# First causal attention of a layered kernel: its row sums' reciprocals spread through DRAM, TensorE's order in groups of up to three steps, and other places for its first tiles and for later layers' loads

## The chip, the cores and the metric

The kernel runs on one core of a Trainium2 chip. Its time is the device time of one execution in microseconds; the time before is the median of three executions.

## The reference

Eight layers are applied to x of 4 batches, 1024 positions and 128 features, each with a residual: an attention, a mixture of experts, a gated attention unit, the same mixture again, a state space layer, a gated feed-forward layer, a second attention, and the feed-forward layer again. The change is in the first attention, with 16 heads of 64 features, all in float32:

```python
q, k, v = split_heads(x @ Wq), split_heads(x @ Wk), split_heads(x @ Wv)   # x is layer-normalized
scores = einsum('bhid,bhjd->bhij', q / sqrt(64), k)       # 1024 x 1024 for each batch and head
attn = softmax(where(causal, -inf, scores), axis=-1)      # key j > query i is masked
out = einsum('bhij,bhjd->bhid', attn, v)                  # heads joined, then @ Wo + bo
```

## The kernel before

**Tiles.** Positions lie on the 128 partitions, in blocks of 128 (`NC` = 8 for each batch). The work is done for a pair of heads `n` at a time: 8 pairs for each of 4 batches, 32 in all, since the features of two heads fill 128 partitions. For a pair, `gq` (0 to 3) counts units of two query blocks (`Q` = 2). A unit has `gq` + 1 steps, and each step takes two key blocks.

**First stage** (`probabilities`, L344 to L387). For each query block TensorE makes scores `s` (L358) of both heads against up to 512 keys, into a PSUM tile of two banks (`ps_s`, 2 buffers). VectorE adds the mask, negates, writes `p` and keeps the row's least value (L364). ScalarE takes the exponential in place and sums the row (L373). When a unit's two query blocks are done, VectorE takes the reciprocals `r` of the sums (L379), and POOL splits them into three bfloat16 parts (L382 to L385).

**Second stage** (`outputs`, L410 to L471). For each step TensorE transposes the blocks of `p` into `t` (L422, a PSUM tile of one bank for each key block, 2 buffers). ScalarE and VectorE copy them to `pt` (L427, L429). TensorE multiplies them with the values into `o` (L460): the first head's features on the lower 64 partitions, the second's on the upper. The reciprocals must lie along `o`'s free dimension and be the same on all 64 partitions of a head: TensorE transposes `parts` (L442), ScalarE copies them (L443), and TensorE multiplies them with a selection matrix `sel` (L452) into the second half of `o`'s bank. ScalarE copies that (L468), and VectorE multiplies it with the product (L469).

**The order.** `pe = k.order()` pins TensorE's instructions to the order in which the code issues them; the other engines' order is a scheduler's. In each step of `outputs` come the transposes of this step, one piece, the spread of the reciprocals if it is waiting, `ahead()`, and then the products of the step before. `ahead()` issues scores of later units until they lead by 20 blocks of 128 x 128 (`LEAD`). A piece is a small job from a list: the projections of pair n + 2 to q, k (L288) and v (L299), the product with Wo for pair n - 1 (L326), and transposes of the normalized x (L268) and of the result (L336). Each piece uses the one PSUM bank of `ps_m`, as the transpose of `parts` does. A batch is normalized (`normalize`, L104 to L119) two pairs before its first.

**The start.** The constructors of all layers run first. They issue the loads of all weights, nearly all on SP's queue, with W1 and W2 of the mixture (2 MB each) among them. Three integer weights of the feed-forward layer are loaded to tiles that are given back at once, and converted on VectorE (L1299). ScalarE and VectorE make `a` of the state space layer (L1046, L1047). The attention's own tiles are taken after that, and `a_one` lies where the given-back tiles lay; the first tiles taken from it are `ident_b`, `mask` and `sel`.

Of the kernel before, what the change touches and what calls it, by code (L numbers as in the profile page):

```python
# [61 lines left out]
class Kernel:  # L62


    def __init__(self, ctx: ExitStack, tc: tile.TileContext, ins: dict, out):
# [13 lines left out]
        self.turn = 0  # L79

    def load(self, pool, name, shape=None, src=None, dtype=F32, engine=None):

        ap = self.ins[name] if src is None else src
        t = pool.tile(list(shape or ap.shape), dtype, name="w_" + name)
        (engine or self.nc.sync).dma_start(t, ap)
        return t
# [15 lines left out]
    def normalize(self, out, in_, n=NC):  # L104
# [4 lines left out]
        for c in range(n):  # L109
            nc.vector.bn_stats(stats[:, c, :], in_[:, c, :])  # L110
        for c in range(n):
            nc.vector.bn_aggr(mv[:, c, :], stats[:, c, :])
        rstd = self.small.tile([P, n], F32, tag="rstd", name="rstd")
        nc.scalar.activation(rstd, mv[:, :, 1], AF.Sqrt, bias=self.eps)
        nc.vector.reciprocal(rstd, rstd)
        for c in range(n):
            nc.vector.tensor_scalar(
                out[:, c, :], in_[:, c, :], mv[:, c, 0:1], rstd[:, c : c + 1], ALU.subtract, ALU.mult
            )  # L119
# [68 lines left out]
class AttentionA:  # L188
# [10 lines left out]

    Q = 2  # L200
    NQ = NC // 2
    NS = 3
# [12 lines left out]
    def __call__(self, start=None):  # L215
        k, tc, nc = self.k, self.k.tc, self.k.nc
        wq, wk, wv, wo, bo = self.wq, self.wk, self.wv, self.wo, self.bo
        Q, NQ, NS, NP = self.Q, self.NQ, self.NS, HEADS // 2
        scale = 1.0 / math.sqrt(DH_A)
        with self.stack as ctx:  # L220
            one = ctx.enter_context(tc.tile_pool(name="a_one", bufs=1))
            sb = ctx.enter_context(tc.tile_pool(name="a_sb", bufs=2))
            ps_s = ctx.enter_context(tc.tile_pool(name="a_ps", bufs=2, space=PSUM))
            ps_t = ctx.enter_context(tc.tile_pool(name="a_pt", bufs=2, space=PSUM))
            ps_o = ctx.enter_context(tc.tile_pool(name="a_po", bufs=1, space=PSUM))
            ps_m = ctx.enter_context(tc.tile_pool(name="a_pm", bufs=1, space=PSUM))
            pe = k.order()

            ident_b = one.tile([P, P], BF16, name="ident_b")
            make_identity(nc, ident_b)  # L230

            mask = one.tile([P, T], BF16, name="mask")
            nc.gpsimd.memset(mask, 0.0)
            nc.gpsimd.affine_select(
                out=mask[:, T - P :], in_=mask[:, T - P :], compare_op=ALU.is_ge, fill=MASKED, base=0,
                pattern=[[-1, P]], channel_multiplier=1,
            )

            rows = NS * 2 * Q
            sel = one.tile([DH_A, Q, P], BF16, name="sel")  # L240
            nc.vector.memset(sel, 0.0)
            for i in range(Q):
                for h in range(2):
                    to = sel[:rows, i, h * DH_A : (h + 1) * DH_A]
                    for part in range(NS):
                        at = (part * 2 + h) * Q + i
                        nc.vector.tensor_tensor(
                            to, to, ident_b[:rows, at : at + 1].to_broadcast([rows, DH_A]), ALU.add
                        )

            turned_parts = [one.tile([DH_A, P], BF16, name=f"turned_parts{n}") for n in range(2)]
            for t in turned_parts:
                nc.vector.memset(t, 0.0)
# [3 lines left out]
            def normalized(b):  # L257
                xl = one.tile([P, NC, C], F32, tag="xl", name="xl")
                k.normalize(xl, k.xb(b))
# [3 lines left out]
                xts[b] = sb.tile([P, T], F32, tag="xt", name="xt")  # L263

                def turned(h):
                    ps = ps_m.tile([P, 512], F32, tag="m", name="ps")
                    for c in range(4):
                        pe(nc.tensor.transpose(ps[:, c * P : (c + 1) * P], xl[:, h * 4 + c, :], k.ident))  # L268
                    k.evacuate(xts[b][:, h * 512 : (h + 1) * 512], ps)
# [74 lines left out]
            def probabilities(n, gq):  # L344

                q, kk = pairs[n]["q"], pairs[n]["k"]
                p = one.tile([P, 2, Q, (gq + 1) * Q * P], F32, tag=f"p{gq}", name="p")
                tops = sb.tile([P, 2, Q, 2], F32, tag="tops", name="tops", bufs=3)
                sums = sb.tile([P, 2, Q], F32, tag="sums", name="sums")
                for i in range(Q):  # L350
                    ib = gq * Q + i
                    width = (ib + 1) * P
                    for at, lo in enumerate(range(0, width, 512)):
# [8 lines left out]
                        m = mask[:, T - hi + lo :] if hi == width else mask[:, : hi - lo]  # L362
                        for h in range(2):
                            nc.vector.tensor_tensor_reduce(  # L364
                                p[:, h, i, lo:hi], s[:, h, : hi - lo], m, -1.0, 3.4e38, ALU.add, ALU.min,
                                tops[:, h, i, at : at + 1],
                            )
# [4 lines left out]
                    for h in range(2):  # L372
                        nc.scalar.activation(  # L373
                            p[:, h, i, :width], p[:, h, i, :width], AF.Exp, bias=tops[:, h, i, 0:1],
                            scale=-1.0, accum_out=sums[:, h, i : i + 1],
                        )
                    if i == Q - 1:
                        r = sb.tile([P, 2, Q], F32, tag="r", name="r")
                        nc.vector.reciprocal(r, sums)  # L379
                        parts = sb.tile([P, NS, 2, Q], BF16, tag="parts", name="parts", bufs=4)  # L380
                        rest = sb.tile([P, 2, Q], F32, tag="rest", name="rest")
                        nc.gpsimd.tensor_copy(parts[:, 0], r)  # L382
                        nc.gpsimd.tensor_tensor(rest, r, parts[:, 0], ALU.subtract)
                        nc.gpsimd.tensor_copy(parts[:, 1], rest)
                        nc.gpsimd.tensor_tensor(parts[:, 2], rest, parts[:, 1], ALU.subtract)  # L385
                        units[n, gq] = p, parts
# [21 lines left out]
            before, waiting = [], []  # L408

            def outputs(n, gq):  # L410


                p, parts = units.pop((n, gq))
                last = (gq + 1) * Q - 1
                for step in range(gq + 1):
                    products = []
                    for jb in (2 * step, 2 * step + 1):
                        lo = max(0, jb * P - gq * Q * P)
                        t = ps_t.tile([P, 2, Q * P], F32, tag="t", name="t")
                        for h in range(2):  # L420
                            for i in range(lo // P, Q):
                                pe(nc.tensor.transpose(  # L422
                                    t[:, h, i * P : (i + 1) * P], p[:, h, i, jb * P : (jb + 1) * P], k.ident
                                ))
                        pt = sb.tile([P, 2, Q * P], F32, tag=f"pt{jb % 2}", name="pt")
                        if jb % 2:
                            nc.scalar.copy(pt[:, :, lo:], t[:, :, lo:])  # L427
                        else:
                            nc.vector.tensor_copy(pt[:, :, lo:], t[:, :, lo:])  # L429
                        products.append((jb, lo, pt))  # L430
                    done[1] += 4 if step < gq else 3
                    if pieces:
                        pieces.pop(0)[1]()
                    while before:
                        before.pop(0)()
                    ahead()
                    while waiting:
                        waiting.pop(0)()
                    if step == 0:
                        o = ps_o.tile([P, 2, Q * P], F32, tag="o", name="o")  # L440
                        ps = ps_m.tile([rows, P], BF16, tag="m", name="ps")
                        pe(nc.tensor.transpose(ps, parts.rearrange("p s h i -> p (s h i)"), ident_b))  # L442
                        nc.scalar.copy(turned_parts[gq % 2][:rows], ps)  # L443
                        before.append(lambda: spread(o, turned_parts[gq % 2]))
                    waiting.append(
                        lambda products=products, step=step: product(n, gq, o, products, last, step == gq)
                    )

            def spread(o, shares):

                for i in range(Q):
                    pe(nc.tensor.matmul(  # L452
                        o[:, 1, i * P : (i + 1) * P], sel[:, i, :], shares, start=True, stop=True
                    ))

# [1391 lines left out]
```

## Time and profile before

| | |
|---|---|
| median of 3 executions (lowest, highest) | 3414.72 us (3413.31, 3426.27) |
| the profiled execution | 3444.67 us, its span 3443.0 us |
| granted TensorE clock over the span | 0.949 |
| first attention | to about 1270 us of the span |
| DMA, 0 to 20 / 34 to 50 us | 250 / 277 GB/s |
| exponentials (L373) | 512 of 768 ns |
| score reductions (L364) | 768 of 553 ns |
| copies of `pt`, VectorE / ScalarE | 320 of 686 ns / 320 of 493 ns |

How to read the profile: PE is TensorE, PEld its weight loads, DVE is VectorE, ACT is ScalarE, POOL is GpSimd and SP the queue that issues most loads. A group of instructions is named by the line in the kernel, the engine, the operation and "output<-inputs". Matmuls are pipelined and their ends are modelled, so the distance between two starts says more than a duration. A float32 matmul with 64 or 128 output rows stands as two records, a transpose as one. The chain of work that ended last is followed back from the last instruction to what released it.

### The profile page before, as it was taken

To read this page: it belongs to the slowest core of one execution; us is meant where nothing else is said; L and a number is where in the kernel's file an instruction comes from. 1 tells how busy PE (TensorE), PEld (TensorE's weight loads), DVE (VectorE), ACT (ScalarE), POOL (GpSimd) and SP (SyncE) were. 2 spreads that over 40 slices of the span, in tenths; PEclk is the share of its full clock that TensorE was granted. 3 is DMA by queue.
4 is the path that set the end of the run, shared out by engine and by line. 5 is a ranking of instruction groups with operands and counts; after the bars stand their busy time and mean duration, and the time that the engine had idled before them with its cause. 6 is when DMAs were issued, how large, how long until landed. Compare 5 with 4: busy or idle time off the path is not lost.

```text
span 3443.0 us, 46496 instructions
## 1 busy us (share of the span) xinstructions
PE 3053.6 (89%) x17008; PEld 1682.7 (49%) x17008; DVE 2318.3 (67%) x5299; ACT 1876.3 (54%) x4074; POOL 367.6 (11%) x780
## 2 busy tenths in 40 slices
PE   4999999999999989869988777979778799999988
PEld 2555555555555547635466434544445344444435
DVE  4666666666666665666566389797978677676634
ACT  3555555555555543335523488879763255655662
POOL 1001000100000001440013300000001111010000
PEclk9999999999999989989999889999999799998999
DMA  5000000000000000110001111111111111111100
GB/s 149 1 1 1 1 1 1 1 1 1 1 1 1 1 1 23 34 36 1 0 13 33 48 55 56 56 50 61 55 50 33 33 43 48 41 51 30 30 2 25
DMA packets 61477, 92.34 MB, mean 27 GB/s; under 512 B 20080, under 2 KB 42368, under 8 KB 58816
## 3 DMA queue, kind: packets, MB, share of 16 engines
q1 hardware_dynamic: 42368, 59.97, 5.5%
q0 software_dynamic: 17408, 27.32, 3.1%
q8 instruction: 133, 2.18, 0.3%
q10 hardware_dynamic: 1472, 2.10, 0.2%
q14 instruction: 96, 0.79, 0.1%
HBM read 73.98 MB, written 15.34 MB: 26 GB/s over the span
## 4 chain that ended last, share of the span: by engine, by line
PE 70%; DVE 10%; ACT 10%; issue 5%; DMA 2%; POOL 1%; another core or an unknown queue 1%; SPq 0%; DVEq 0%; ACTq 0%; POOLq 0%
PE s L358 9%; PE o L460 8%; PE t L422 8%; PE acc L1240 4%; PE o L1626 4%; PE acc L662 4%; PE ps L288 4%; PE x L1592 3%; PE s L1528 3%; PE acc L961 3%; ACT p L1598 3%; PE py L695 2%; PE ps L684 2%; ACT hc L1239 2%; PE ps L326 2%
## 5 line engine op out<-in xcount | busy, mean ns | idle before, releaser
L364 DVE CUSTOM_DVE_ANT_0 p<-s,mask 128x512 f32<-128x512 f32 (+3 forms) x768 | 395.1, 553 | 187.6 <-PE s L358 187.1
L1598 ACT ACTIVATE p<-x 128x512 f32<-128x512 f32 (+3 forms) x768 | 337.7, 490 | 250.4 <-PE x L1597 180.7
L1537 DVE TENSOR_REDUCE tops<-s 128x2 f32<-128x1024 f32 (+3 forms) x384 | 361.2, 955 | 134.7 <-PE s L1533 94.1
L373 ACT ACTIVATE p<-p,tops 128x640 f32<-128x640 f32 (+7 forms) x512 | 391.9, 768 | 108.7 <-DVE tops L371 83.9
L1240 PE MATMUL acc<-hc,ident 128*128 128x512 f32 x512 | 271.0, 653 | 90.5 <-ACT hc L1239 89.8
L358 PE MATMUL s<-kt,qt 64*128 64x512 f32 (+3 forms) x1536 | 344.3, 527 | 1.2 <-DVE tops L364 1.2
L422 PE MATMUL t<-ident,p 128*128 128x128 f32 x2304 | 322.2, 281 | 0.0
L460 PE MATMUL o<-pt,vv 128*64 128x256 f32 (+1 forms) x2560 | 319.6, 371 | 0.0
L1227 DVE TENSOR_TENSOR_SCAN st<-decay,st 128x1024 f32<-128x1024 f32 x128 | 288.7, 2278 | 10.8 <-ACT decay L1224 10.2
L427 ACT COPY pt<-t 128x512 f32<-128x512 f32 (+1 forms) x320 | 157.7, 493 | 247.0 <-PE t L422 246.9
L422 PEld LDWEIGHTS t<-ident,p 128*128 128x128 f32 x2304 | 245.8, 141 | 87.8 <-issue 45.3
L460 PEld LDWEIGHTS o<-pt,vv 128*64 128x64 f32 x2560 | 155.4, 136 | 245.6 <-issue 199.0
L429 DVE COPY pt<-t 128x512 f32<-128x512 f32 x320 | 219.4, 686 | 61.7 <-PE t L422 61.7
L1592 PE MATMUL x<-q,k 75*128 75x512 bf16 (+3 forms) x768 | 224.1, 339 | 27.7 <-ACT p L1598 15.0
L1528 PE MATMUL s<-k,q 72*128 72x512 bf16 (+3 forms) x768 | 217.8, 350 | 28.4 <-DVE tops L1537 17.5
L1239 ACT ACTIVATE hc<-ps,by_time 128x256 f32<-128x256 f32 x512 | 200.2, 477 | 48.6 <-PE ps L1233 48.5
L1240 PEld LDWEIGHTS acc<-hc,ident 128*128 128x128 f32 x512 | 91.6, 198 | 206.2 <-ACT hc L1239 187.3
L1226 DVE TENSOR_TENSOR st<-du,bs 128x1024 f32<-128x1024 f32 x128 | 151.8, 1216 | 46.8 <-PE ps L1233 46.7
L1233 PEld LDWEIGHTS ps<-ident,st 128*128 128x128 f32 x1024 | 128.0, 148 | 97.9 <-issue 60.5
L1626 PE MATMUL o<-p,vx 128*32 128x512 f32 (+3 forms) x1536 | 173.3, 523 | 0.0
L358 PEld LDWEIGHTS s<-kt,qt 64*128 64x128 f32 x1536 | 119.3, 188 | 108.5 <-issue 69.3
L751 POOL DMA_INDIRECT got<-y_rows,rows x128 | 135.8, 1061 | 319.2 <-DMA y_rows<-y 202.0
(285 smaller groups left out, 5011.3 us busy)
## 6 DMA issues: line engine op xcount, KB each, us to landing
bs<-b_rows SPq DMA_DIRECT2D x64, 512.0 KB
k<-b_parts POOLq DMA_DIRECT2D x16, 576.0 KB
q<-b_parts POOLq DMA_DIRECT2D x48, 192.0 KB
b_parts<-part SPq DMA_DIRECT2D x24, 256.0 KB
y_rows<-y SPq DMA_DIRECT2D x16, 192.0 KB
x<-in_x_dram SPq DMA_DIRECT2D x4, 512.0 KB
w_W<-in_W_dram SPq DMA_DIRECT2D x1, 2048.0 KB
y_rows<-y SPq DMA_DIRECT2D x8, 256.0 KB
```

The costliest lines, as they stand in the source:

```text
L358: pe(nc.tensor.matmul(s[:, h, : hi - lo], q[feats, ib * P : (ib + 1) * P], kk[feats, lo:hi], start=True, stop=True,))
L364: nc.vector.tensor_tensor_reduce(p[:, h, i, lo:hi], s[:, h, : hi - lo], m, -1.0, 3.4e38, ALU.add, ALU.min, tops[:, h, i, at : at + 1],)
L373: nc.scalar.activation(p[:, h, i, :width], p[:, h, i, :width], AF.Exp, bias=tops[:, h, i, 0:1], scale=-1.0, accum_out=sums[:, h, i : i + 1],)
L422: pe(nc.tensor.transpose(t[:, h, i * P : (i + 1) * P], p[:, h, i, jb * P : (jb + 1) * P], k.ident))
L460: pe(nc.tensor.matmul(o[feats, 0, lo:], pairs[n]["v"][:, jb, feats], pt[:, h, lo:], start=jb == 0, stop=jb == last,))
L1227: nc.vector.tensor_tensor_scan(st, decay, st, 0.0, ALU.mult, ALU.add)
L1240: nc.tensor.matmul(acc[:, c : c + 2, :].rearrange("p c d -> p (c d)"), k.ident, hc.rearrange("p c d -> p (c d)"), start=n == 0, stop=n == ...
L1528: start.pin(nc.tensor.matmul(s[:, a, : hi - lo], qq[:ROWS, two + a, ib * P : (ib + 1) * P], kk[:ROWS, two + a, lo:hi], start=True, stop=ha ...
L1537: nc.vector.tensor_reduce(tops[:, half, two : two + 2, n], s[:, :, : hi - lo], AX.X, ALU.max)
L1592: start.pin(nc.tensor.matmul(x[:, lo:], kk[:FULL, a, jb * P : (jb + 1) * P], qq[:FULL, a, hq * 512 + lo : (hq + 1) * 512], start=True, sto ...
L1598: nc.scalar.activation(p[:, a, lo:], x[:, lo:], AF.Exp)
L1626: start.pin(nc.tensor.matmul(o[a * VW : (a + 1) * VW, lo:], vx[b % 2][:, jb, first : first + VW], p[:, a, lo:], start=jb == 0, stop=jb == ...
```

## The change

Line numbers with the word "changed" are those of the changed file.

- **Reciprocals.** `parts`, `sel`, `turned_parts`, `ident_b` and the matmuls and copies on them are gone. SP writes `r` to a DRAM tile with its positions contiguous, then loads each head's row of 256 back to 64 partitions, as `share` (changed L383 to L391). VectorE multiplies `o` with it (changed L432).
- **TensorE's turns.** The steps of a unit are taken in groups: 1, 2, 3, and 2 + 2 for `gq` = 0 to 3. A group has a piece, all its transposes, a second piece, `ahead()`, and then its own products, without waiting for the next step. Transposes and scores share one pool of three PSUM tiles of two banks each. `pt` has three buffers.
- **VectorE's order.** The score reductions and the instructions of `normalize` are pinned in the order of the code.
- **First tiles.** `p` of `gq` = 3 has a pool of its own (`a_late`), taken first, so that it lies where the integer weights lay. The mask has 640 columns in place of 1024, and `xt` has one buffer.
- **Later layers' loads.** W1, W2 and the exponential for `a` are issued by ScalarE behind the first exponential of `gq` = 2, and VectorE's part of `a` follows. The integer weights are converted on POOL.

```diff
@@ Kernel @@
+    def load_late(self, pool, name, shape, src):
+        t = pool.tile(shape, F32, name="w_" + name)
+        self.late.append(lambda: self.nc.scalar.dma_start(t, src))
+        return t
...
-    def normalize(self, out, in_, n=NC):
+    def normalize(self, out, in_, n=NC, pin=lambda ins: ins):
...
-            nc.vector.bn_stats(stats[:, c, :], in_[:, c, :])
+            pin(nc.vector.bn_stats(stats[:, c, :], in_[:, c, :]))
...
@@ AttentionA @@
-    NS = 3
+    GROUPS = [[(0,)], [(0, 1)], [(0, 1, 2)], [(0, 1), (2, 3)]]
...
+            late = ctx.enter_context(tc.tile_pool(name="a_late", bufs=1))
             one = ctx.enter_context(tc.tile_pool(name="a_one", bufs=1))
             sb = ctx.enter_context(tc.tile_pool(name="a_sb", bufs=2))
-            ps_s = ctx.enter_context(tc.tile_pool(name="a_ps", bufs=2, space=PSUM))
-            ps_t = ctx.enter_context(tc.tile_pool(name="a_pt", bufs=2, space=PSUM))
+            dram = ctx.enter_context(tc.tile_pool(name="a_dram", bufs=6, space=DRAM))
+            ps_s = ctx.enter_context(tc.tile_pool(name="a_ps", bufs=3, space=PSUM))
             ps_o = ctx.enter_context(tc.tile_pool(name="a_po", bufs=1, space=PSUM))
             ps_m = ctx.enter_context(tc.tile_pool(name="a_pm", bufs=1, space=PSUM))
-            pe = k.order()
+            pe, ve = k.order(), k.order()
...
-                k.normalize(xl, k.xb(b))
+                k.normalize(xl, k.xb(b), pin=ve)
...
-                            nc.vector.tensor_tensor_reduce(
+                            ve(nc.vector.tensor_tensor_reduce(
...
+                    if k.late and gq == 2:
+                        pin = k.order()
+                        pin(exp)
+                        while k.late:
+                            pin(k.late.pop(0)())
+                        while k.late_v:
+                            ve(k.late_v.pop(0)())
                     if i == Q - 1:
                         r = sb.tile([P, 2, Q], F32, tag="r", name="r")
                         nc.vector.reciprocal(r, sums)
-                        parts = sb.tile([P, NS, 2, Q], BF16, tag="parts", name="parts", bufs=4)
...
-                        units[n, gq] = p, parts
+                        there = dram.tile([2, Q, P], F32, tag="shares", name="shares")
+                        nc.sync.dma_start(there.rearrange("h i p -> p h i"), r)
+                        share = sb.tile([P, Q * P], F32, tag="share", name="share", bufs=4)
+                        for h in range(2):
+                            nc.sync.dma_start(
+                                share[h * DH_A : (h + 1) * DH_A],
+                                there[h : h + 1].rearrange("h i p -> h (i p)").to_broadcast([DH_A, Q * P]),
+                            )
+                        units[n, gq] = p, share
...
+                p, share = units.pop((n, gq))
+                o = ps_o.tile([P, Q * P], F32, tag="o", name="o")
+                for steps in self.GROUPS[gq]:
+                    piece()
+                    blocks = [block for step in steps for block in turned(p, gq, step)]
+                    piece()
                     ahead()
-                    while waiting:
-                        waiting.pop(0)()
...
+                    for block in blocks:
+                        product(n, gq, o, *block)
+                if gq == 0:
+                    pairs[n]["o"] = sb.tile([P, T], F32, tag="ot", name="ot")
+                nc.vector.tensor_tensor(
+                    pairs[n]["o"][:, gq * Q * P : (gq + 1) * Q * P], o, share, ALU.mult
+                )
+
+            def turned(p, gq, step):
+
+                t = ps_s.tile([P, 2, 2, Q * P], F32, tag="s", name="t")
...
+                    pt = sb.tile([P, 2, Q * P], F32, tag=f"pt{m}", name="pt", bufs=3)
...
@@ Mixture, StateSpace, GatedFFN @@
-        self.w1 = k.load(w, "W1", [P, NEXP, FF], k.ins["W1"].rearrange("e c h -> c e h"))
-        self.w2 = k.load(
+        self.w1 = k.load_late(w, "W1", [P, NEXP, FF], k.ins["W1"].rearrange("e c h -> c e h"))
+        self.w2 = k.load_late(
...
-        nc.scalar.activation(a, per[:, :, D_CONV + 3 :], AF.Exp)
-        nc.vector.tensor_scalar(a, a, -1.0, None, ALU.mult)
+        k.late.append(lambda: nc.scalar.activation(a, per[:, :, D_CONV + 3 :], AF.Exp))
+        k.late_v.append(lambda: nc.vector.tensor_scalar(a, a, -1.0, None, ALU.mult))
...
-            k.nc.vector.tensor_scalar(t, whole, float(np.float32(1.0 / 127.0)), None, ALU.mult)
+            k.nc.gpsimd.tensor_scalar(t, whole, float(np.float32(1.0 / 127.0)), None, ALU.mult)
```

## The prediction

> **What bounds the kernel now.** I read the page's first rows, then the busy time of the stretch of this layer, then the chain that ended last over its first 60 us, then TensorE's timeline in its steady part, and last the waits.
>
> ```profile
> span 3443.0 us, 46496 instructions
> PE 3053.6 (89%) x17008; PEld 1682.7 (49%) x17008; DVE 2318.3 (67%) x5299; ACT 1876.3 (54%) x4074; POOL 367.6 (11%) x780
> ```
>
> ```profile
> 600.00:900.00 300.00, 292.05 (x1864) 157.51 (x1864) 201.80 (x624) 168.73 (x426) 27.00 (x129) 1.00 0.00 1
> ```
>
> Columns of the second: the stretch, its length, then busy us of PE, PEld, DVE, ACT and POOL, TensorE's granted clock, DMA share, GB/s. In this layer (about 54 to 1265 us) TensorE is busy 97% of the time, VectorE 67%, ScalarE 56%, DMA not at all. So the end of this stage is set by TensorE's own row of work, and a pair of heads takes 37.6 us (300 us hold 1864 matmul records at 234 for each pair).
>
> The start is bound otherwise:
>
> ```profile
> 23.78 5.05 DMA w_wgT<-in_wgT_dram
> 29.34 2.35 DMA w_wuT<-in_wuT_dram
> 32.18 3.38 DMA w_wdT<-in_wdT_dram
> 37.55 1.77 DVE sel L247 x12
> 43.31 2.09 PE ps L288 x2
> 53.76 2.47 PE s L358 x9
> ```
>
> (start, us, what.) The chain runs through the three integer weights of a later layer: their conversions (L1299) stand on VectorE ahead of the first `xl`, and ident_b waits for them on POOL. The normalization was ready at 10.4 us (ScalarE's first root), but the first scores come at 53.76.
>
> TensorE in the steady part (start, duration, instruction; I take the distance from one start to the next):
>
> ```profile
> 1191.57 1.13 PE L358 MATMUL s<-kt,qt 64*128 64x512 f32 x4
> 1192.63 0.87 PE L460 MATMUL o<-pt,vv 128*64 128x256 f32 x8
> 1193.43 0.22 PE L442 MATMUL ps<-ident_b,parts 128*12 128x128 bf16 x1
> 1193.58 1.09 PE L422 MATMUL t<-ident,p 128*128 128x128 f32 x8
> 1195.53 1.13 PE L288 MATMUL ps<-xt,w_Wk 128*128 128x512 f32 x2 [0.85 <-ACT turned_parts L443]
> 1196.59 0.23 PE L452 MATMUL o<-turned_parts,sel 64*128 64x128 bf16 x1
> ...
> 1196.71 1.07 PE L358 MATMUL s<-kt,qt 64*128 64x512 f32 x3
> 1197.71 1.08 PE L460 MATMUL o<-pt,vv 128*64 128x256 f32 x8
> 1198.73 1.09 PE L422 MATMUL t<-ident,p 128*128 128x128 f32 x8
> 1199.66 1.02 PE L288 MATMUL ps<-xt,w_Wq 128*128 128x512 f32 x2
> 1200.61 1.35 PE L358 MATMUL s<-kt,qt 64*128 64x128 f32 x8
> 1201.89 1.08 PE L460 MATMUL o<-pt,vv 128*64 128x256 f32 x8
> ```
>
> **A turn has a price of its own.** Products of 512 columns take 1.02, of 384 (the diagonal step at 1192.63) 0.80: 0.22 for 128 columns, 1.67 ns a column, so 0.17 is fixed. Scores of 512 columns take 1.06, two tiles of 640 together 1.28: again 0.22, so 0.21 is fixed, once for the turn and not for each tile. Eight transposes take 0.93 and six 0.71 before a piece (from the same timeline): 0.107 each and 0.08 fixed. A piece of 512 columns takes 0.95: 0.10 fixed. One step (transposes, piece, scores, products) thus carries 0.56 us that is no column; without a piece 0.55 (transposes straight to scores 0.17).
>
> **The change part by part.**
>
> *Groups of steps.* Steps per pair go from 1+2+3+4 = 10 to 5 groups; over 32 pairs 320 turns become 160: 160 x 0.55 = -88 us. Columns stay the same.
>
> *Reciprocals.* TensorE loses 128 transposes of `parts` at 0.15 (1193.43 to 1193.58) = -19, and 128 pairs of `sel`: a score turn with them takes 1.12 (1196.59 to 1197.71) against 1.06: 0.06 each, -8. With `parts` goes the wait for its bank:
>
> ```profile
> PE ps L288 <- ACT turned_parts L443: 24.8, 30, 0.9
> PE ps L442 <- ACT qt L290: 4.2, 3, 1.4
> ```
>
> (us, times, longest), -29. ScalarE's 128 share copies (47.6 us) and turned_parts copies (31.5), and POOL's 512 splits were beside TensorE: nothing. Sum so far -144.
>
> *What the new order adds on TensorE.* A piece now also stands between products and transposes. The trace shows products to a piece once (1.67 for 896 columns, 0.18 fixed, like products to transposes) and never a piece to transposes: 0 to 0.1, I take 0.05 for some 112 of them: +6. Transposes and scores now share three tiles. Laying out two pairs by hand with the durations above, 0.61 for a VectorE reduction of 512 (L364), 0.69 for its copy, 0.58 for ScalarE's, 1.13 for an exponential of 1024, I find two stalls in every pair. In the group of three steps the fourth score tile (384) needs the first one's (512) two reductions, which end 0.65 us later than TensorE is there. In the first group of gq 3 the second piece needs the bank whose copy (qt, ScalarE) stands behind two exponentials of 1024, three more of 128 and 256, and two of 384: 0.4 to 0.7. With 0.1 for gq 0: 1.2 a pair, +38. Ends: 0 (the order slips so that VectorE is ahead) and 2.4.
>
> *Normalization pinned.* Before, statistics of all batches ran in VectorE's idle start. Now the pin holds those of batches 1 to 3 at their place: eight bn_stats (1.65), aggregates (0.62), then the root on ScalarE behind the last exponentials and a table load (1.28 + 0.30), then `xl` (2.1), and the very next instruction on TensorE is the transpose of `xl`. TensorE is there about 5 us early, three times: +16. Ends: 6 (VectorE partly ahead) and 24.
>
> *Start.* Conversions go to POOL, L1047 and ScalarE's exponential of `a` move behind p2, the last score tile p3 alone lies where the integer weights lay. Then nothing is between the root and `xl`: first xl at 10.9, all eight at 13, second half of xt at 14.9 (the same steps took 40.86 to 43.31), scores 10.4 later as now: 25.4 against 53.76, -28. Wq had landed (row_bo at 9.31 on SP waits for its queue slot, and went on by 12.8). p3's first reduction, at about 37, waits for POOL's last conversion; w_wdT lands at about 36.5, POOL needs 0.5 to 0.9 (its copy of 960 takes 0.98): about even. W1 and W2 (4 MB) are issued by ScalarE at about 35 instead of 33.6 by SP; they fill the DMA engines to about 50 (34 to 50 us shows 277 GB/s now), and the first mixture needs them at 1308: hidden. But the first two shares are written at 35, behind SP's weight issues, into that traffic: back at about 43, needed at 38.6, and VectorE's queue (copies of `vv` and `pt`) stands behind that multiply: +4. Start -24, ends -28 and -14.
>
> *Shares through DRAM.* Per unit SP issues a write of 512 single elements, waits for it, and issues two loads; 384 issues. The nearest row is SP's rows_there (L1561) and its reload: 2721.09 to 2722.49, 1.4 us from issue to landed. Single elements cost more: queue q1's 42368 packets took 5.5% of 16 engines' span, 71.5 ns each; 512 over 16 engines: 2.3. So 1.4 + 2.3 + two issues 0.7 each + 1.4 = 6.5 us. The Trainium skill speaks against this form: "DMA: Bandwidth & Descriptors", section Rules for kernel authors, says that a non-contiguous last dimension becomes one descriptor per element, and its section Anatomy of one DMA gives about 2.0 us fixed for a DMA: by it 7.7. The tightest unit (gq 3) is issued when its last exponential is done, some 14 us before its multiply; gq 0 to 2 have 15 to 20. By row or rule the trip is hidden. If not, VectorE stands at the multiply, with the next transposes' copies behind it.
>
> *A second rule against.* "TensorE: Matmul & The Clock Gate", Part 4, says that transposes do not count as busy for the clock in the same way, and Part 1 that it is judged by windows of 3.4 us. Runs grow from 8 (0.85 us) to 22 (2.35). If the clock halved for one window in the four long groups of a pair, that were 4 x 1.7 x 32 = +218. The row shows a granted 1.00 with a fifth of the time in transposes, and 2.35 does not fill a window: I take 0.
>
> *The rest.* Behind this layer the instructions of VectorE, ScalarE and POOL stand in the same order. 0.
>
> Sum: -88 -19 -8 -29 +6 +38 +16 -24 = -108. The profiled execution took 3444.67 us (span 3443.0 and 1.7 around it), 30 above the median of 3414.72; the change is in a stage of granted clock 1.00, so I take the difference over: 3444.7 to 3337, and the median to **3307**.
>
> **The rivals.**
> - *The stalls don't appear* (score tiles and copies slip past each other): without the +38 and 10 less for the pins, 3259 to 3275, say 3269. For it: VectorE stays at 73% (25.1 of 34.4 us a pair). Chance 0.14.
> - *Three shared tiles and one bank couple the engines*: a further 0.4 us in each of 5 groups, +64: 3371. For it: ScalarE's exponentials come in bursts of 6 us with the piece's copy behind them. Chance 0.14.
> - *Slower: the shares come late.* SP takes the units one by one, and keeps up while issue, landing and reissue take less than 34.4/4 = 8.6 us; I have about 5. If the write is spread over 4 engines instead of 16 (9.2 for 2.3), SP takes 12: 128 x 3.4 = +435 less 108, 3742; from 9.4 us a unit on the change loses. Against: rows_there is of the same form and landed in 1.4. Chance 0.08 with the clock.
> - *It does half*: the start doesn't move, since other loads stand ahead: 3331. Within the first case's spread, 0.1 of its 0.64.
>
> **Numbers.** Likeliest 3307 (0.64); 3269 (0.14), 3371 (0.14), slower (0.08). Its own range is 3280 to 3340; the range 3262 to 3365 takes in the bounds of the stalls and most of both neighbours. A measurement here tells about 0.5% (17 us) from no change: faster 0.89 and same 0.03 (the far end of the 3371 case), slower 0.08.
>
> **What would show it.** No L442 and L452; score and product turns 160 and not 320, with the same 1.67 ns a column; first scores near 25 us; a pair in about 34.4 us; a wait of TensorE on the reduction before a 384 tile and on qt of 0.5 us each; three gaps of 5 us at `xl`. Waits of L432 on a share's DMA after the first pair, a granted clock under 0.95, or VectorE over 85% would prove me wrong.

## The result, and the profile after

| | median of 4 executions (lowest, highest) | ratio to before, 95% interval |
|---|---|---|
| before | 3415.89 us (3413.31, 3426.27) | |
| after | 3667.59 us (3664.24, 3672.32) | 1.0732 (1.0706 to 1.0757) |

The kernel became 252 us slower, where 108 us less had been forecast. The profiled execution of the changed kernel took 3672.3 us, its span 3670.3. All of the loss lies in the first attention: its last addition to x (L338 before, L331 after) starts at 1270.4 us before and at 1522.3 after, 251.9 us later.

The page's first rows and one of its groups (busy us, mean ns | idle time of the engine just before, and what ended most of it), after:

```profile
span 3670.3 us, 45502 instructions
PE 3041.5 (83%) x16624; PEld 1703.2 (46%) x16624; DVE 2321.3 (63%) x5281; ACT 1827.0 (50%) x3819; POOL 272.2 (7%) x269
...
L445 PE MATMUL t<-ident,p 128*128 128x128 f32 x2304 | 359.3, 286 | 272.1 <-DVE pt L452 271.3
```

The steady stretch, in the columns that the prediction explains, after:

```profile
600.00:900.00 300.00, 237.47 (x1458) 134.24 (x1454) 169.68 (x523) 128.55 (x295) 2.35 (x1) 0.98 0.10 13
```

TensorE was busy 292 us of such a stretch before, now 237; VectorE and ScalarE do less too. So no engine has become the bound: the engines wait for each other. A stretch holds 1458 matmul records; with 222 to a pair of heads (234 less the 12 of `parts` and `sel`) a pair takes 45.7 us, where 34.4 had been forecast. The group says at what: TensorE stood 271 us in front of transposes until VectorE's copy L452 was done. The timeline shows where, in a group of three steps, after:

```profile
622.69 0.66 PE L445 MATMUL t<-ident,p 128*128 128x128 f32 x4
624.13 1.09 PE L445 MATMUL t<-ident,p 128*128 128x128 f32 x8 [0.78 <-DVE pt L452]
626.01 1.09 PE L445 MATMUL t<-ident,p 128*128 128x128 f32 x8 [0.78 <-DVE pt L452]
627.88 0.44 PE L445 MATMUL t<-ident,p 128*128 128x128 f32 x2 [0.78 <-DVE pt L452]
628.25 1.78 PE L353 MATMUL s<-kt,qt 64*128 64x512 f32 x12
630.79 0.92 PE L353 MATMUL s<-kt,qt 64*128 64x384 f32 x4 [0.76 <-DVE tops L359]
```

The transposes no longer come in rows of 8 (0.93 us from start to start before) but stop in the middle of each step. From one stop to the next are 1.88 us; that is 8 transposes and about 1 us of waiting. The first row is the four transposes of a step's first key block; then TensorE waits for VectorE's copy of that block, and only then come the four of the second block (and, without a stop, the first four of the next step). VectorE's timeline has that copy, which ends at 624.07, just ahead of TensorE's row of 624.13:

```profile
623.38 0.69 DVE L452 COPY pt<-t 128x512 f32<-128x512 f32 x1 [0.15 <-PE t L445]
```

This is 320 steps of about 1 us. TensorE's waits from 100 to 1400 us (us, times, longest), after:

```profile
PE t L445 <- DVE pt L452: 230.9, 281, 1.3
PE s L353 <- DVE tops L359: 18.7, 27, 0.8
PE ps L261 <- DVE xl L124: 13.9, 3, 4.9
```

The second and the third are the forecast's stall in the group of three and its gaps at `xl`. The first is in no step of the forecast.

At the start the first scores stand at 23.96 us (53.76 before, 25.4 forecast). What follows took most of that back; ScalarE's timeline, after:

```profile
34.81 0.40 ACTq L94 DMA_DIRECT2D w_W<-in_W_dram  x1
47.29 0.02 ACT L94 MOVE_SHAPE w_W<-in_W_dram  x1 [14.47 <-DMA w_b<-in_b_dram]
...
50.09 0.35 ACT L450 COPY pt<-t 128x256 f32<-128x256 f32 x1
```

and TensorE's, after:

```profile
50.49 0.69 PE L460 MATMUL o<-pt,vv 128*64 128x128 f32 x4 [10.26 <-ACT pt L450]
...
61.22 1.97 PE L445 MATMUL t<-ident,p 128*128 128x128 f32 x8 [7.18 <-DVE pt L452]
```

ScalarE issued W1, then stood 12 us at the issue of W2 until an earlier load (`w_b`, queued on SP at 35 us, into W1's traffic) had landed, with a copy of `pt` behind it that TensorE needed. The second wait hides a share: VectorE's multiply L432 waited until 59.5 for a share whose write had been issued at 36.2, and L452 stood behind it. TensorE came to the second half of the first transposes of `gq` = 1 at 61.2 us; the kernel before began these transposes at 65.5. Of the 30 us at the first scores about 4 were left.

**Theory A**: the two halves of `t` are one tile, and TensorE's write to the second half is made to wait for VectorE's read of the first, though the two lie in different banks. Rivals: B, the trips through DRAM and loads; C, three shared PSUM tiles are too few.

### The profile page after: what moved, and what is told of

Its sections match the earlier page's. It is cut to its first block, busy times and chain, and to the rows that moved or that the text cites. A ratio compares the mean times of both kernels' runs of the same rounds, so it can differ in the third digit from the quotient of the medians.

```text
span 3670.3 us, 45502 instructions
## 1 busy us (share of the span) xinstructions
PE 3041.5 (83%) x16624; PEld 1703.2 (46%) x16624; DVE 2321.3 (63%) x5281; ACT 1827.0 (50%) x3819; POOL 272.2 (7%) x269
## 4 chain that ended last, share of the span: by engine, by line
PE 63%; DVE 19%; ACT 7%; issue 6%; DMA 4%; POOL 1%; SPq 0%; DVEq 0%; ACTq 0%; POOLq 0%
PE t L445 8%; PE s L353 7%; PE o L460 7%; DVE pt L452 6%; PE o L1614 4%; PE acc L650 4%; PE acc L1228 4%; PE x L1580 3%; PE ps L281 3%; PE s L1516 3%; PE acc L949 3%; ACT p L1586 2%; PE ps L319 2%; ACT hc L1227 2%; PE ps L292 2%
## 5 line engine op out<-in xcount | busy, mean ns | idle before, releaser
L445 PE MATMUL t<-ident,p 128*128 128x128 f32 x2304 | 359.3, 286 | 272.1 <-DVE pt L452 271.3
L445 PEld LDWEIGHTS t<-ident,p 128*128 128x128 f32 x2304 | 259.4, 143 | 408.2 <-DVE pt L452 348.8
L452 DVE COPY pt<-t 128x512 f32<-128x512 f32 x320 | 220.4, 689 | 248.0 <-PE t L445 246.3
L353 PE MATMUL s<-kt,qt 64*128 64x512 f32 (+3 forms) x1536 | 315.6, 531 | 20.9 <-DVE tops L359 20.7
L460 PE MATMUL o<-pt,vv 128*64 128x256 f32 (+1 forms) x2560 | 288.7, 368 | 10.3 <-ACT pt L450 10.3
L460 PEld LDWEIGHTS o<-pt,vv 128*64 128x64 f32 x2560 | 171.2, 138 | 185.3 <-issue 106.3
L353 PEld LDWEIGHTS s<-kt,qt 64*128 64x128 f32 x1536 | 128.5, 196 | 185.3 <-issue 125.2
L650 PE MATMUL acc<-d,xl 128*128 128x480 f32 (+1 forms) x384 | 154.5, 564 | 26.7 <-DVE d L645 26.7
```

Source lines behind the costliest of these rows:

```text
L353: pe(nc.tensor.matmul(s[:, h, : hi - lo], q[feats, ib * P : (ib + 1) * P], kk[feats, lo:hi], start=True, stop=True,))
L445: pe(nc.tensor.transpose(t[:, m, h, i * P : (i + 1) * P], p[:, h, i, jb * P : (jb + 1) * P], k.ident))
L452: nc.vector.tensor_copy(pt[:, :, lo:], t[:, m, :, lo:])
L460: pe(nc.tensor.matmul(o[feats, lo:], pairs[n]["v"][:, jb, feats], pt[:, h, lo:], start=jb == 0, stop=jb == (gq + 1) * Q - 1,))
```

## The experiments

All medians in us; "before" was run beside each (3417.18, 3416.86, 3416.11 and 3417.12 for the four groups below, in order).

| run | median | ratio to before, 95% interval |
|---|---|---|
| e1, copies behind all transposes | 3395.93 | 0.9937 (0.9914 to 0.9961) |
| e2, tiles of one bank | 3386.62 | 0.9913 (0.9886 to 0.9939) |
| e3, before with a two-bank tile | 3709.48 | 1.0863 (1.0837 to 1.0889) |
| e4, e1 and loads later | 3376.79 | 0.9887 (0.9858 to 0.9917) |
| f1, e4 and share loads on POOL | 3622.42 | 1.0608 (1.0583 to 1.0632) |
| f2, e4 without the trip | 3311.36 | 0.9701 (0.9681 to 0.972) |
| f3, e4 in single steps | 3678.32 | 1.0761 (1.0731 to 1.079) |
| f4, e4 with the normalization free | 3452.28 | 1.0109 (1.0074 to 1.0144) |
| g1, f2 with the normalization free | 3297.04 | 0.9655 (0.9634 to 0.9677) |
| g2, f2 in single steps | 3448.33 | 1.0097 (1.0069 to 1.0125) |
| g3, e4 with writes of 16 bytes | 3312.47 | 0.9701 (0.9672 to 0.973) |
| g4, e4 with the multiply on POOL | 3331.84 | 0.9745 (0.9718 to 0.9771) |
| h1, f4 with writes of 8 bytes | 3296.3 | 0.965 (0.9633 to 0.9666) |
| h2, before with the shares alone | 3372.85 | 0.9867 (0.985 to 0.9883) |
| h3, before with the start alone | 3402.87 | 0.9957 (0.994 to 0.9974) |
| i1, after with writes of 16 bytes | 3652.72 | 1.0693 (1.0675 to 1.0711) |

### The wait, from both sides: e1, e2, e3

e1 moves the two copies of a step behind its transposes, in the same tile:

```diff
                             pe(nc.tensor.transpose(
                                 t[:, m, h, i * P : (i + 1) * P], ...
                             ))
+                for m in range(2):
+                    jb = 2 * step + m
+                    lo = max(0, jb * P - gq * Q * P)
                     pt = sb.tile([P, 2, Q * P], F32, tag=f"pt{m}", name="pt", bufs=3)
```

> The changed kernel, with both copies of a step issued behind all its transposes. Theory A: in the changed kernel the second half's transposes wait for VectorE's copy of the first half, since both halves are one tile, 1.03 us in each of 320 steps. Then this one gives 300 to 330 us back: 3340 us (3310 to 3390), distance from 8 transposes to 8 transposes 0.9 to 1.0 us instead of 1.9, TensorE waiting on L452's successor almost only for score tiles. Theory B: the loss comes from the trips through DRAM and the loads in flight: nothing given back, 3640 to 3680. Theory C: three shared tiles of two banks bind TensorE, whoever reads: the wait moves from the transposes to the scores, 3550 to 3670.

e2 keeps the order half, copy, half, copy, and gives each half (and each head's scores) a tile of one bank:

```diff
-                t = ps_s.tile([P, 2, 2, Q * P], F32, tag="s", name="t")
...
                 for m in range(2):
+                    t = ps_s.tile([P, 2, Q * P], F32, tag="s", name="t")
```

> The changed kernel in its own order (half, copy, half, copy), but each half and each head's scores in a PSUM tile of one bank of its own, six of them in the pool. Theory A (one tile for two halves is what makes the wait): 3340 us (3300 to 3390), as without the order. If the order of issue alone made the wait, it would stay: 3640 to 3680. Theory C (a lack of banks): six smaller tiles are the same banks, so 3550 to 3670.

e3 is the kernel before, and puts its two key blocks into one tile:

```diff
-                        t = ps_t.tile([P, 2, Q * P], F32, tag="t", name="t")
+                    t2 = ps_t.tile([P, 2, 2, Q * P], F32, tag="t", name="t")
...
+                        t = t2[:, jb % 2]
```

> The kernel before, with only this changed: the two key blocks of a step share one PSUM tile of two banks (one buffer) in place of two tiles of one bank; order and work as before. Theory A: TensorE waits 1.0 us for VectorE's copy in each of 320 steps, some 320 us: 3740 us (3650 to 3770). Theories B and C, in which the loss is not in this wait: 3405 to 3440.

e1 gives 272 us back, e2 281, and e3 loses 292 from a kernel that has no other part of the change. The same group of three in e1:

```profile
626.86 2.56 PE L445 MATMUL t<-ident,p 128*128 128x128 f32 x22
629.26 1.02 PE L319 MATMUL ps<-ot,w_Wo 128*128 128x512 f32 x2
630.22 1.78 PE L353 MATMUL s<-kt,qt 64*128 64x512 f32 x12
632.76 0.92 PE L353 MATMUL s<-kt,qt 64*128 64x384 f32 x4 [0.76 <-DVE tops L359]
633.61 2.60 PE L463 MATMUL o<-pt,vv 128*64 128x256 f32 x24
```

22 transposes start to start in 2.40 us, where the changed kernel took 5.56 (622.69 to 628.25, without the piece). And in e3 the wait that the kernel before never had (its timeline, then its waits from 100 to 1400 us):

```profile
612.57 0.66 PE L423 MATMUL t<-ident,p 128*128 128x128 f32 x4
614.01 0.66 PE L423 MATMUL t<-ident,p 128*128 128x128 f32 x4 [0.78 <-DVE pt L430]
```

```profile
PE t L423 <- DVE pt L430: 226.7, 277, 1.5
```

In e2 TensorE's row runs on to 621.83 while VectorE copies out of banks that the row has just filled (TensorE's timeline, then VectorE's):

```profile
619.43 2.57 PE L445 MATMUL t<-ident,p 128*128 128x128 f32 x22
```

```profile
620.24 1.40 DVE L452 COPY pt<-t 128x512 f32<-128x512 f32 x2
```

So theory A is shown: both the shared tile (e2) and the copy issued between the halves (e1) are needed for the wait, and they make it without the rest of the change (e3). Rival C falls with e1: the same three tiles. The different banks did not need the wait: the Trainium skill ("PSUM — Partial Sum Buffer", section PSUM bank collisions raise a hardware error) asks for a guard by bank and quadrant, and e2 runs with writer and reader in different banks at once. That the wait is put into the program where one tile is shared follows from these runs; the semaphores of the built program themselves are not shown here.

Yet e1 missed its own expectation by 56 us. Rival B was dismissed too early, as the next runs show.

### Loads later: e4

```diff
-                    if k.late and gq == 2:
+                    if k.late and n == 1 and gq == 2:
```

> As the first of these (copies behind), and W1, W2 and the exponential of a issued in the second pair's third unit in place of the first pair's. Theory: ScalarE stood from 34.8 to 47.3 us at the issue of W2, with copies of pt behind it, and the first shares were written into W1's traffic and took to 59.6; with the loads later TensorE's stops of 10.3 and 7.2 us go: 15 us less than the first of these (10 to 20), and the second unit's transposes stand near 45 us in the span instead of 61. Rival: the loads cost the same where they stand later: 0 to 4 us less.

19.1 us less than e1, a little over the 15 expected. One of the two stops stayed: TensorE's transposes of 37.85 are followed by a stop of 10.8 us to 50.35, behind VectorE, which stood 10.4 us for a write of `r` to land (the buffer of `r` was needed again) and 2.6 us more for the first share. So the loads' place was worth 19 us, and the first shares are late with W1 out of the way too.

### The trip: f1, f2, g3, g4, i1

With TensorE's wait gone, a wait on the trip had come up. VectorE's waits from 100 to 1270 us, e1:

```profile
DVE ot L432 <- DMA share<-shares: 83.0, 23, 10.6
...
DVE r L381 <- DMA shares<-r: 48.2, 25, 3.9
```

Behind the multiply stand the copies of `pt`; TensorE's longest stop in e1 (7.32 us at 200.78, released by a copy) follows on VectorE's wait of 10.64 us for a share at 199.02.

f1 lets POOL issue the loads of a share (`nc.gpsimd.dma_start` for `nc.sync.dma_start` at changed L387) and gives `r` four buffers:

> As the run with copies behind and loads later, and each share's two loads are issued by POOL in place of SP, with four buffers for r in place of two. Theory: with TensorE's wait gone a unit takes 8.6 us and SP, which stands 6.6 us at each unit's landing write and issues three transfers, about as long, so that VectorE waited 88 us for shares and 47 us for r's buffer, and TensorE some 32 us for copies behind them. With SP free of the landing these go: 35 us less (25 to 45), 3342 us, VectorE's wait for shares under 15 us. Rival: the trip itself is too long, whoever issues it: 3370 to 3400 us, the same waits.

Wrong by 280 us. VectorE waits 215 us for shares instead of 88 and TensorE stops for 7 us about once a pair. In one such pair `r` was made at 441.80 and POOL issued the loads at 455.81, 14 us later. In f1 SP no longer stands at a write, and a write can be on its way together with loads that another queue has issued. What makes the trip longer was not settled.

f2 replaces the trip by a constant tile, so the reciprocals are not spread:

```diff
-                        there = dram.tile([2, Q, P], F32, tag="shares", name="shares")
-                        nc.sync.dma_start(there.rearrange("h i p -> p h i"), r)
...
+                        share = share_one
```

> As the run with copies behind and loads later, but no trip: VectorE multiplies o with a constant tile (the spread of the reciprocals is left out, the reciprocals themselves are still made). It gives what the trip costs in all, start included. Theory: 45 us less than with the trip (32 at TensorE's waits for copies, 11 at the start), 3332 us (3320 to 3345). Rival, the trip is hidden and the rest of the gap to the forecast lies elsewhere: 3370 to 3380 us.

65 us less than e4: the trip's price, more than expected, and the time is 4 us from the forecast of the whole change. TensorE's waits in the stage are the forecast's two (21.0 us at the fourth score tile, 13.9 at `xl`), and the pairs of heads take 33.3 and 35.4 us in turn, 34.4 in the mean, as forecast.

g3 keeps the trip and changes only the form of its write; it leaves out the reordering that would put each share at its own position, so its shares stand at other positions:

```diff
-                        nc.sync.dma_start(there.rearrange("h i p -> p h i"), r)
+                        nc.sync.dma_start(
+                            there.rearrange("h i p -> (h i p)").rearrange("(p k) -> p k", k=2 * Q),
+                            r.rearrange("p h i -> p (h i)"))
```

> As the run with copies behind and loads later (3377 us), but r is written to DRAM as it lies, 128 pieces of 16 bytes in place of 512 single elements, so that the shares hold the right numbers at other positions. Theory: the number of elements makes the write's 6.6 to 6.9 us to landing and SP's 8.6 us a unit; then the landing falls to about 3 us, SP's wait from 752 to some 350 us, VectorE's wait for shares from 88 to under 30, and the time to 3330 us (3315 to 3345). Rival: the landing is a fixed price of a write and its completion, whatever its pieces: 3370 to 3380, SP's wait within 50 us of 752.

64 us less than e4 and within 1 us of f2: all of the trip's price was in writing 512 single elements. SP's wait for the write to land (80 to 1300 us: us, times, longest), first e4, then g3:

```profile
SPq L387 <- DMA shares<-r: 751.9, 113, 15.1
```

```profile
SPq L387 <- DMA shares<-r: 102.0, 79, 6.2
```

That is 6.7 us for each wait against 1.3. (SP often issues two writes one behind the other. For writes that stand alone its timeline has 8.4 us in the mean from the end of the write's issue to the first load's in e4, and 1.5 in g3.) With the write's issue (0.53) and the two loads' (1.08) SP had 8.3 us of work in a unit of 8.6: it could just follow, but a unit that was late stayed late.

g4 takes TensorE out of reach of a late share instead: VectorE copies `o`, POOL multiplies later, and `joined` is queued at `gq` = 2.

> As the run with copies behind and loads later (3377 us), but VectorE copies o as it is, POOL multiplies the copy with the share when that has landed, the products with Wo are queued one unit later, and r has four buffers. Nothing but POOL waits for a trip. Theory: TensorE's 32 us of waits for copies and 11 us at the start go, as in the run without a trip: 3320 us (3308 to 3335). Rival: SP can't keep up at 8.6 us a unit, POOL's multiply comes late for the product with Wo, or POOL slows VectorE: 3350 us or more.

3331.84, within what was expected, 20 above f2: 9.5 us of it at the layer's end, where the last product waits for POOL, and 5.7 at `qt`.

i1 is the changed kernel with g3's write (and g3's order of the shares):

> The changed kernel with r written as it lies (128 pieces of 16 bytes, so that the shares hold the right numbers at other positions), and nothing else: TensorE's wait for the copy stays. Theory: at 11.3 us a unit the trip was covered but for the start, so 0 to 15 us less than the changed kernel: 3655 us (3645 to 3668), though the same edit took 64 us from the kernel without the wait. Rival: the trip costs 64 us here too, 3604 us.

15 us less than the changed kernel, where the same edit took 64 from e4. At 11 us a unit the wait in the transposes had covered most of the trip: transposes that start at 86.29 us in the changed kernel start at 80.03 in i1, 6 us of the 15, and from 66 to 1400 us VectorE's waits for shares and for `r`'s buffer come to 9 us in the changed kernel.

### Turns and pins: f3, f4, g1, g2

f3 and g2 make each step its own group; f4 and g1 leave out `pin=ve`; g1 and g2 stand on f2.

```diff
-    GROUPS = [[(0,)], [(0, 1)], [(0, 1, 2)], [(0, 1), (2, 3)]]
+    GROUPS = [[(j,) for j in range(gq + 1)] for gq in range(4)]
```

> As the run with copies behind and loads later, but every step is a group of its own, so 320 turns in place of 160. Theory of the forecast: a turn has a price of 0.55 us, so 88 us more: 3465 us (3450 to 3490, above that if the copies of one step are no longer covered). Rival, that turns are free and the forecast's 88 us were never there: within 15 us of 3377.

> As the run with copies behind and loads later, with the instructions of the normalization free on VectorE as before. Theory: TensorE's three waits at xl, 13.9 us in all, go: 14 us less, 3363 us (3355 to 3370). Rival: the free statistics stand ahead of reductions elsewhere, 3370 to 3385.

Both wrong: 302 us more, and 75 more where 14 less was expected. In both VectorE's wait for shares had grown (183 and 158 us against 88), so neither edit was priced by itself. Hence the two without the trip:

> As the run without the trip (3311 us; the spread of the reciprocals is left out), with the normalization's instructions free on VectorE. It takes the pin's price apart from the shares, since without pins and with the trip TensorE's waits at xl went but VectorE's wait for shares grew from 88 to 158 us. Theory: 14 us less than 3311, 3297 us (3290 to 3303), no wait at xl. Rival, the free statistics are what costs, with or without a trip: 3330 us or more.

> As the run without the trip (3311 us; the spread of the reciprocals is left out), with every step a group of its own: 320 turns in place of 160. With the trip in place single steps cost 301 us, of which shares and copies are a part. Theory of the forecast: 0.55 us a turn, 88 us, and on top what the copies of a step are no longer covered: 3400 us bare, 3400 to 3500 with that; turns' starts show the same fixed parts. Rival: a turn's price is over 1 us, 3550 or more.

g1: 14.3 us less than f2. g2: 137 more. Its waits of TensorE for copies (80 to 1300 us):

```profile
PE o L458 <- ACT pt L448: 51.5, 86, 2.7
...
PE o L458 <- DVE pt L450: 6.7, 19, 0.8
```

58 us are copies no longer covered. f2's 21 us at the fourth score tile are gone in g2, so what is left for the 160 turns lies between 79 and 100 us, 0.49 to 0.62 us for each, against 0.55 in the forecast. One turn of g2 without a piece (from the scores at 609.50 to those at 612.63) takes 3.13 us; less 1024 columns at 1.67 ns and 8 transposes at 0.107 us that is 0.56.

### Parts of the change alone, and a better version: h1, h2, h3

h2 is the kernel before with the change's DRAM lines in place of `parts`, `sel` and their work, and the mask of 640 columns. h3 is the kernel before with the start's part.

> The kernel before with the trip through DRAM alone: parts, sel, ident_b and their work gone, three instructions on SP for each unit as in the change, the mask of 640 columns, all else as before. The forecast: 56 us less than before (19 + 8 + 29), 3360 us, if the trip is hidden. Theory now: a unit takes some 9 us there and SP 8.6, so part of the gain is lost to shares that come late: 3375 us (3355 to 3400). Rival, the trip is longer than the old order's slack everywhere: 3430 or more.

> The kernel before with the start's part alone: p of gq 3 in a pool of its own, W1, W2 and the exponential of a behind the first exponential of gq 2 on ScalarE, integer weights converted on POOL, mask of 640 columns, one buffer of xt. The forecast: 28 us less at the first scores, 24 in the sum: 3392 us. Theory now: ScalarE stands 12 us at the issue of W2 with copies behind it, so 14 to 18 less: 3400 us (3393 to 3407). Rival: nothing is left, 3410 to 3420.

44 and 14 us less than before: both close to what was expected. h2's VectorE waits 14 us for shares and 43 for `r`'s buffer: in the old order, at some 9 us a unit, the trip was nearly hidden. Neither run is one part alone: h2 has no `sel` at its start and has its first scores 2.5 us earlier (51.20), and h3 still makes `sel` ahead of them and has them at 33.91, not at 24.

h1 is f4 with the two query blocks of a row side by side in DRAM:

```diff
-                        there = dram.tile([2, Q, P], F32, tag="shares", name="shares")
-                        nc.sync.dma_start(there.rearrange("h i p -> p h i"), r)
+                        there = dram.tile([2, P, Q], F32, tag="shares", name="shares")
+                        nc.sync.dma_start(there.rearrange("h p i -> p h i"), r)
...
+                    share.rearrange("f (p i) -> f i p", i=Q), ALU.mult,
```

> Copies behind, loads later, the normalization free, and the shares laid out in DRAM with a row's two query blocks side by side: 256 writes of 8 bytes in place of 512 of 4, and VectorE reads the share with a stride. Theory: the landing falls from 6.9 to about 4.2 us (between 2.9 for 128 pieces and 6.9 for 512), SP has room, the shares wait nowhere, and the pins' 14 us are gone as in the run without a trip: 3298 us (3292 to 3310). Rival: the landing is still too long or the strided multiply slows VectorE: 3320 us or more.

3296.3 us: 3.5% less than before (ratio 0.965, 0.9633 to 0.9666), and within 1 us of g1, which has no trip; h1 leaves nothing of the reference out. SP waits 2.3 us each time (242.8 us, 106 times), VectorE's strided multiply still takes 0.42 us, and TensorE's granted clock from 300 to 1100 us is 1.00.

## Why the prediction was wrong, point by point

- **The step that failed: "Columns stay the same", and "*Groups of steps*" with it.** The forecast took a step's transposes as a row of eight at 0.93 us, as in the kernel before. The change also puts both key blocks into one tile of two banks, with the first block's copy issued between them, and the forecast counted only how many tiles there are, not who waits inside one. Price: 272 (e1), 281 (e2), 292 us (e3). The rival of the three shared tiles had a coupling of the engines too, but at 64 us and through ScalarE's bursts; e1 has the same tiles and not the loss. The trace of the changed kernel shows this wait at the first transpose of each second half, 0.78 us for each in the group shown and about 1 us by the starts.
- **Shares, "hidden, 0": wrong in size.** The forecast took 1.4 + 2.3 us for the write to land; SP waited 6.7 in the mean, 8.4 behind a write that stands alone. "SP takes the units one by one ... I have about 5" was 8.3. The row that the 1.4 came from is not "of the same form", as the forecast has it: L1561 writes 48 contiguous rows of 256 bytes, and g3's contiguous write indeed waits 1.3 to 1.5. So the size that failed is the 2.3 for the single elements: 5.4 to 6.9 by the difference of e4 and g3. While the main fault stood, the write's form cost 15 us (i1); without it, 64 (g3). The rival "the shares come late" named this wait, but 8.3 us is still under its limit of 8.6, and it was not what made the kernel slower: that the kernel came out slower, as this rival had it, is luck. The rule of the Trainium skill that the forecast weighed and set aside ("DMA: Bandwidth & Descriptors", section Rules for kernel authors: a non-contiguous last dimension becomes one descriptor per element) was the right warning: the form of the write alone is worth 64 us. (The 2.0 us that it took from the section Anatomy of one DMA are that page's fit for DMAs issued by GpSimd; these writes are SP's, and no run here shows their fixed part alone.)
- **Start, -24.** The first scores came as forecast. Unforeseen was that ScalarE stands 12 us at the issue of W2, which had been counted as an issue without a wait ("hidden"): putting the loads later gives 19 us (e4). In the old order, where W2's issue did not stand, the start's part gave 14 (h3, with `sel` still ahead of the first scores).
- **Turns, -88 at 0.55**: 0.49 to 0.62 by the times of g2 and f2 (-79 to -100), 0.56 by the starts. **Parts, `sel` and bank, -56**: -44 in h2, with the trip's lateness and 2.5 us of an earlier start in it. **Pins, +16**: 14.3 (g1), 13.9 in the trace.
- **Stalls of 1.2 us a pair, +38**: in e1 the group of three takes 3.39 us for its scores where 1280 columns at 1.67 ns and 0.21 make 2.35, so 1.04 where 0.65 was forecast. The other, at `qt`, is 0.07 instead of 0.4 to 0.7. The sum was right, its parts were not.
- **Clock, 0**: 22 transposes in 2.40 us and a granted clock of 1.00 in the stage (f2, h1): the fear of longer runs of transposes did not come true.
- **Together.** In this order, 3667.6 less the wait (271.7), the loads (19.1) and the form of the write (64.3) is 3312.5, the time of g3, against 3307 forecast. The unpriced wait, the loads and the write are all of the error but 6 us. That the other terms together came so near is in part luck: single ones are off by up to 12 us (`parts`, `sel` and bank in h2; turns, at the upper end), and go both ways.

## What to carry to other kernels

When a change merges two buffers into one, list who waits inside the merged tile: a reader of one half can hold up the writer of the other, although they use different banks. Here this one wait was worth more than all the terms of the forecast's sum together. And price an edit again after the main fault is gone: the trip cost 15 us under it and 64 without it, and two experiments (f3, f4) measured the trip along with what they were made for.

## What was not expected of the hardware

- Behind a DRAM write of 512 single float32 elements from SBUF SP waited 6.7 us in the mean, behind 256 pieces of 8 bytes 2.3, and behind 128 of 16 bytes 1.3 (e4, h1, g3); for writes that stand alone 8.4, 3.0 and 1.5. All three write 2 KB. From 256 to 512 pieces the wait nearly trebles; why was not settled.
- A recorded wait can stand beside a modelled duration that is too short: e2 shows no wait in the group of three (`s` from 622.78 to 626.15, 3.37 us), e1 one of 0.76 us (3.39 us). Only the distance from start to start told that both lose the same.
